# A 3x3 spatial convolution computed in pairs of rows: input-row sums on POOL, four products instead of six, combined on ACT and VectorE

## The chip, the core and the metric

The kernel runs on one core of a Trainium2 chip. A core has five engines with a queue of instructions each: PE (TensorE, matrix products), ACT (ScalarE), DVE (VectorE), POOL (GpSimd) and SP (SyncE, which here only issues DMA transfers). Each queue is worked off in order. PE reads SBUF and writes PSUM, a small memory of eight banks of 128 x 512 f32. The metric is the device time of one launch in microseconds (us).

## What is computed

Two layers work on x of shape (4, 128, 64, 64) in f32. Layer 0 is multi-head attention over the 4096 positions of each image, followed by a residual and a layer norm over channels. Layer 1 adds three branches of the result: a 3x3 convolution over 128 channels, a 1x1 product in the frequency domain, and a Mamba block (a selective scan over the positions).

```python
x = _L0_conv_ref(x, Wq, bq, Wk, bk, Wv, bv, Wo, bo, gamma, beta)   # 4 heads of 32, softmax over 4096 keys
spatial = jax.lax.conv_general_dilated(x, conv_spatial_w, (1, 1), ((1, 1), (1, 1)),
    dimension_numbers=('NCHW', 'OIHW', 'NCHW')) + conv_spatial_b[None, :, None, None]
ym = _mamba(u, in_proj_w, conv1d_w, conv1d_b, x_proj_w, dt_proj_w, dt_proj_b, A_log, D, out_proj_w)
...
return spatial + spectral + ym
```

The change concerns `spatial` alone.

## The kernel before

The work is cut into 32 chunks of 512 positions: a chunk is 8 rows of 64 of one image, held as 128 channels x 512. One Python loop writes the instructions of all engines in one order, in steps of a counter t. The attention takes 2048 steps: 64 halves (a half is a chunk of queries and a pair of heads) of 32 steps each, so that 64 steps belong to one chunk. In this document "step p" is the step with t mod 64 = p.

Each attention step issues to PE, in this order: six products into `s2` that end in the scores for the exponential (L496), four products into `s1` for the maxima of a later half (L455), then the products of other jobs, then two products of the exponentials of the step before with the values, `po` (L516). ACT takes the exponential of `s2` (L504, `e`), DVE reduces `s1` to maxima (L462, `part`). `s1` and `s2` have one buffer each of two banks, so that PE's next products into them wait for DVE and ACT. Every two steps there is also one state of the scan: ACT makes the decay `dA` (L829), POOL the input term `db` (L834), DVE scans (L846, `hs`), POOL multiplies by C and adds to an accumulator (L856, L875). On the last step of a half, `oz` (L526 on ACT, L527 on DVE) empties `po`. When the attention is over (`late`), the scan of the last chunks goes on alone, with `db` on DVE and the sum over states on PE (L882).

Everything else is a job: a generator that yields what it needs next, namely "P", "D" or "A" (a place on PE, DVE or ACT in this step), "B" (one of two PSUM banks), or "" (only the next step). `Plan.step` gives the places out by rank. An odd step has two places for each of PE, DVE and ACT, an even one has one place on ACT.

`convolve(c)` is such a job, of rank 3, queued at t0 + SLOT + 30. It takes one bank and issues nine products of 128 x 512, one per tap, with the padded input `xp` (10 rows of 66) read at an offset of dy rows and dx columns, one product per place "P". A tenth, `g_hil` with `hx`, adds a part of the spectral branch. Then ACT copies the bank to `ym` with the bias (L940). `scan_output` adds `ym` to the Mamba output about a chunk later (L997). `constants_of_the_rest` prepares the weights once: a part of the spectral 1x1 product is added to the middle tap.

The jobs of one chunk stand in the same steps from chunk to chunk. The products of `convolve` stand in steps 57, 59, 61, 63 and 1, two in each.

Of the kernel before, what the change touches and what calls it, by code (L numbers as in the profile page):

```python
# [9 lines left out]
F32 = mybir.dt.float32  # L10
F32R = mybir.dt.float32r
AF = mybir.ActivationFunctionType
ALU = mybir.AluOpType
# [4 lines left out]
P = 128  # L18
W = 64
# [5 lines left out]
RPC = L // W  # L25
# [136 lines left out]
def attention_then_conv_mamba(  # L162
# [17 lines left out]
    nc = tc.nc  # L180
# [8 lines left out]
    const = ctx.enter_context(tc.tile_pool(name="const", bufs=1))  # L189
    att = ctx.enter_context(tc.tile_pool(name="att", bufs=2))  # L190
    loc = ctx.enter_context(tc.tile_pool(name="loc", bufs=2))
# [9 lines left out]
    for h in range(HEADS):  # L201
        k, j = divmod(h, 2)
# [3 lines left out]
    for h in range(HEADS):  # L206
        k, j = divmod(h, 2)
        c = COL["bk"] + k
# [8 lines left out]
    for h in range(HEADS):  # L217
        k, j = divmod(h, 2)
        c = COL["bq"] + h
# [15 lines left out]
    nc.scalar.dma_start(vec, vecs)  # L235
    cw = const.tile([P, 9, P], F32, name="cw")
    nc.scalar.dma_start(cw, conv_w)
    inw = const.tile([P, 2 * DI], F32, name="inw")
    nc.scalar.dma_start(inw, in_w)

# [13 lines left out]
    def col(name, k=0):  # L254
        return vec[:, COL[name] + k : COL[name] + k + 1]
# [12 lines left out]
    g_flip, g_hil, g_fliphil = (g[:, k, :] for k in range(3))  # L268
# [8 lines left out]
    def constants_of_the_rest():  # L277


        yield ""  # L280
        half = loc.tile([P, 2, 2 * P], F32, tag="sg1", name="half", bufs=1)
        nc.vector.tensor_scalar(half, spw, 0.5, None, ALU.mult)
        rr, ir = half[:, 0, :P], half[:, 0, P:]
        ri, ii = half[:, 1, :P], half[:, 1, P:]
        yield ""
        g_id = loc.tile([P, P], F32, tag="ob", name="g_id", bufs=1)
        nc.gpsimd.tensor_tensor(g_id, rr, ii, ALU.add)
        nc.gpsimd.tensor_tensor(cw[:, 4, :], cw[:, 4, :], g_id, ALU.add)
        nc.gpsimd.tensor_tensor(g_flip, rr, ii, ALU.subtract)
        nc.gpsimd.tensor_tensor(g_hil, ri, ir, ALU.subtract)  # L290
        nc.gpsimd.tensor_tensor(g_fliphil, ri, ir, ALU.add)
        yield ""
        nc.vector.tensor_scalar(sbias, cst[:, K_G : K_G + W], col("spec_bi"), None, ALU.mult)
        nc.vector.tensor_tensor(sbias[:, 0:1], sbias[:, 0:1], col("spec_br"), ALU.add)
        high = loc.tile([4 * DTR, DI], F32R, tag="zg1", name="dtw_high", bufs=1)
        nc.vector.tensor_copy(high, dtw_f)
        nc.vector.scalar_tensor_tensor(dtw, high, less_w[: 4 * DTR], dtw_f, ALU.mult, ALU.add)

        nc.scalar.activation(negA, vec[:, COL["A_log"] : COL["A_log"] + NH * NS], AF.Exp)
        yield ""  # L300
        nc.vector.tensor_scalar(negA, negA, -1.0, None, ALU.mult)


        bank = yield "PB"
        pb = bank_tile(bank, [P, 1], "pb")
        nc.tensor.matmul(pb, Wo, bvc, start=True, stop=True)
        yield "D"
        plan.release(bank, 2)
        nc.vector.tensor_tensor(bo, pb, col("bo"), ALU.add)
# [18 lines left out]
    plan = Plan(2, {"x": 2, "f": 1})  # L328

    def bank_tile(bank, shape, name):  # L330
        return psum.tile(shape, F32, tag=f"m{bank}", name=name)
# [309 lines left out]
    xps, xss, dts, us, accs, gates, xds, bcds = ({} for _ in range(8))  # L641
# [245 lines left out]
    hxs, yms, edges, wd, ymd = {}, {}, set(), {}, {}  # L887
# [31 lines left out]
    def convolve(c):  # L919

        i = c % NCH
        while c not in edges or c not in hxs:
            yield ""
        bank = yield "PB"
        pf = bank_tile(bank, [P, RPC, W], f"pf_{c}")
        for k in range(9):
            if k:
                yield "P"
            dy, dx = divmod(k, 3)
            nc.tensor.matmul(  # L930
                pf, cw[:, k, :], xps[c][:, dy : dy + RPC, dx : dx + W], start=k == 0, stop=False
            )
        flat = pf.rearrange("p r w -> p (r w)")
        yield "P"
        nc.tensor.matmul(flat, g_hil, hxs.pop(c), start=False, stop=True)
        yield "A"
        plan.release(bank)
        ym = loc.tile([P, L], F32, tag="ym", name=f"ym_{c}", bufs=2)
        yms[c] = ym
        nc.scalar.activation(ym, flat, AF.Identity, bias=col("conv_b"))  # L940
        if i == 0:
            nc.gpsimd.tensor_tensor(ym[:, :W], ym[:, :W], sbias, ALU.add)

# [88 lines left out]
    for b in range(B):  # L1032
# [3 lines left out]
        for i in range(NCH):  # L1036
# [3 lines left out]
            plan.at(t0 + NT + 1 + i * TPC, 0, place_v(b, i))  # L1040
    plan.at(-20, 0, constants_of_attention())
    plan.at(-4, 2, constants_of_the_rest())
    for H in range(HALVES):
        if H % PAIRS == 0:
# [5 lines left out]
    for c in range(CHUNKS):  # L1050
        t0 = (c + 1) * SLOT
        plan.at(t0, 0, load_residual(c))
        plan.at(t0 + 16, 1, mamba_input(c))
        plan.at(t0 + SLOT + 30, 3, convolve(c))
        plan.at(c * SLOT + LAG + 6, 3, gate(c))
        plan.at((c + 1) * SLOT + LAG + (2 if c < CHUNKS - 3 else 6), 0, scan_output(c))
# [7 lines left out]
    while t < end or not plan.idle():  # L1064
# [10 lines left out]
        c, s = divmod(t - LAG, SLOT)  # L1075
# [110 lines left out]
```

## Time and profile before

| what | value |
|---|---|
| median of 3 runs | 6019.52 us (6018.47 to 6020.24) |
| the profiled execution | 6019.83 us, its span 6018.0 us, granted clock 0.987 |
| PE busy | 5827.6 us, 97% |
| DVE, ACT, POOL busy | 4292.9, 3550.9, 4481.7 us (71%, 59%, 74%) |
| first and last `e` (L504) | start at 132.3 us and 5796.7 us |
| one chunk (64 steps), middle of the span | 178.8 to 179.1 us |
| after the last `e` starts | 221.3 us, PE busy for 138.9 us of it, DVE 170.8 us, POOL 166.6 us |

Busy time of PE counts a product from its start to its modelled end; products overlap, so the pace is read from one start to the next. "PEld" is the load of weights, which overlaps PE. A line of the timeline gives start, duration, engine, source line, operation, tiles, shapes, the number of instructions merged into it and, in brackets, how long the engine had been idle and what ended that. An f32 product shows as two matrix instructions, each with its own load of weights.

### The profile page before, as it was taken

Reading aid. Unit: us, or ns where it says so; the run is one execution under the profiler, and the core shown is the slowest. Engines: PE = TensorE matmul, PEld = TensorE weight load, DVE = VectorE, ACT = ScalarE, POOL = GpSimd, SP = SyncE. Lnnn points to the kernel's source line nnn. Section 1 sums busy time; section 2 is a strip of 40 time slices with the busy share of each in tenths; the row PEclk is TensorE's granted clock in tenths of the full one; section 3 lists DMA queues with packets and bytes.
Section 4 is the critical chain, followed back from the end, with each engine's and each line's share of the span. In section 5 each row is a group of like instructions: output and inputs, shape, how many; then the busy total and the mean of one; then the engine's idle time right before and its main releaser. Section 6 shows DMA issues by size and latency. Waiting matters only on the chain. (4 is left out here: it accounts for less than half of the span.)

```text
span 6018.0 us, 83940 instructions
## 1 busy us (share of the span) xinstructions
PE 5827.6 (97%) x31126; PEld 2415.4 (40%) x31126; DVE 4292.9 (71%) x4505; ACT 3550.9 (59%) x4762; POOL 4481.7 (74%) x4523
## 2 busy tenths in 40 slices
PE   5999999999999999999999999999999999999976
PEld 2444444444444444444444444444444444444422
DVE  4557777777777777777777777777777777777657
ACT  1455666665666666666666666666566666666653
POOL 0006888778888777888787888877788887788887
PEclk7999999999999999999999999999999999999988
DMA  4012222323333222323433323322333222222233
GB/s 129 21 37 57 67 72 76 72 71 109 84 90 74 75 70 71 76 69 81 110 86 79 77 67 72 76 72 68 110 76 92 68 67 64 67 70 65 60 101 90
DMA packets 423320, 456.46 MB, mean 76 GB/s; under 512 B 203360, under 2 KB 204928, under 8 KB 422912
## 3 DMA queue, kind: packets, MB, share of 16 engines
q1 hardware_dynamic: 418256, 449.23, 29.4%
q8 instruction: 246, 4.03, 0.3%
q10 hardware_dynamic: 4656, 1.87, 0.1%
q14 instruction: 162, 1.33, 0.1%
HBM read 376.21 MB, written 66.32 MB: 74 GB/s over the span
## 5 line engine op out<-in xcount | busy, mean ns | idle before, releaser
L462 DVE TENSOR_REDUCE part<-s 128x2 f32<-128x1024 f32 x2048 | 2498.0, 1221 | 1460.7 <-PE s L455 1460.5
L504 ACT ACTIVATE e<-s 128x1024 f32<-128x1024 f32 x2048 | 2095.0, 1023 | 2176.7 <-PE s L496 2174.2
L516 PE MATMUL po<-e,V 128*33 128x512 f32 x8192 | 2181.9, 605 | 2.7 <-DVE oz L527 0.3
L496 PE MATMUL s<-Q,K 64*128 64x512 f32 x8192 | 1502.9, 444 | 8.8 <-ACT e L504 4.4
L455 PE MATMUL s<-K,Q 64*128 64x512 f32 x8192 | 1320.6, 400 | 47.8 <-DVE part L462 35.9
L856 POOL TENSOR_TENSOR hs<-hs,bc 128x512 f32<-128x512 f32 x948 | 1210.3, 1277 | 170.3 <-DVE hs L846 101.8
L496 PEld LDWEIGHTS s<-Q,K 64*128 64x128 f32 x8192 | 610.4, 185 | 1730.5 <-ACT e L504 1257.1
L834 POOL TENSOR_TENSOR db<-u,bc 128x512 f32<-128x512 f32 x948 | 1215.3, 1282 | 0.0
L875 POOL TENSOR_TENSOR acc<-acc,hs 128x512 f32<-128x512 f32 x894 | 1145.0, 1281 | 70.1
L846 DVE TENSOR_TENSOR_SCAN hs<-dA,state,db 128x512 f32<-128x512 f32 x826 | 1052.2, 1274 | 49.4 <-ACT dA L829 47.7
L455 PEld LDWEIGHTS s<-K,Q 64*128 64x128 f32 x8192 | 751.2, 186 | 313.3 <-DVE part L462 140.6
L496 PE MATMUL s<-MX,sel 64*128 64x512 f32 x4096 | 811.3, 392 | 0.0
L829 ACT ACTIVATE dA<-dt,negA 128x512 f32<-128x512 f32 x1024 | 703.0, 687 | 112.1 <-DVE V L846 69.5
L855 POOL COPY state<-hs 128x1 f32<-128x1 f32 x858 | 158.6, 185 | 769.3 <-DVE hs L846 769.1
L516 PEld LDWEIGHTS po<-e,V 128*33 128x33 f32 x8192 | 305.5, 109 | 906.9 <-issue 862.2
L496 PEld LDWEIGHTS s<-MX,sel 64*128 64x128 f32 x4096 | 386.3, 184 | 91.5 <-issue 0.3
L930 PE MATMUL pf<-xp,cw 128*128 128x512 f32 x576 | 288.8, 620 | 0.0
L560 POOL TENSOR_TENSOR op<-op,rz 128x512 f32<-128x512 f32 x32 | 41.7, 1303 | 184.0 <-DMA rz<-rd 184.0
L846 DVE TENSOR_TENSOR_SCAN hs<-dA,zero,db 128x512 f32<-128x512 f32 x128 | 163.0, 1274 | 0.3
L882 PE MATMUL acc<-V,cst 128*128 128x512 f32 x140 | 92.5, 761 | 64.2 <-POOL V L856 64.1
L930 PEld LDWEIGHTS pf<-xp,cw 128*128 128x128 f32 x576 | 97.0, 189 | 122.3 <-issue 120.9
L714 POOL TENSOR_TENSOR xs<-xs,sg_x 128x512 f32<-128x512 f32 x64 | 82.0, 1281 | 74.8 <-ACT sg_x L638 74.8
(143 smaller groups left out, 3392.8 us busy)
## 6 DMA issues: line engine op xcount, KB each, us to landing
bc<-bcd SPq DMA_DIRECT2D x487, 512.0 KB
Q<-qd SPq DMA_DIRECT2D x256, 128.0 KB
K<-kd SPq DMA_DIRECT2D x64, 256.0 KB
MX<-md SPq DMA_DIRECT2D x1024, 0.5 KB
K<-bcd SPq DMA_DIRECT2D x42, 256.0 KB
vd<-vst SPq DMA_DIRECT2D x32, 264.0 KB
V<-vd SPq DMA_DIRECT2D x32, 264.0 KB
xq<-in_x SPq DMA_DIRECT2D x32, 256.0 KB
```

What stands on the lines that cost most here:

```text
L455: nc.tensor.matmul(sc[:, j, :], QT[H][rows[j], n, t * P : (t + 1) * P], KK[k][m][rows[j], :], start=n == 0, stop=n == 1,)
L462: nc.vector.tensor_reduce(part[H][:, :, t, m], sc, AX.X, ALU.max)
L496: nc.tensor.matmul(s[:, j, :], sel[rows[j], :] if n == 2 else KK[k][i][rows[j], t * P : (t + 1) * P], mov[rows[j], :], start=n == 0, stop= ...
L504: nc.scalar.activation(e, s, AF.Exp)
L516: nc.tensor.matmul(po[H][used[j], :], VA[i][:, t, 2 * k + j, :], e[:, j, :], start=m == 0, stop=m == NT - 1,)
L829: nc.scalar.activation(dA[c, v], dts[c][hf], AF.Exp, scale=negA[:, k : k + 1])
L834: engine.tensor_tensor(db[c, v], us[c][hf], bcs[c, n][0], ALU.mult)
L846: nc.vector.tensor_tensor_scan(hs, dA.pop((c, v)), db.pop((c, v)), state[:, k : k + 1] if c % NCH else zero, ALU.mult, ALU.add,)
L855: nc.gpsimd.tensor_copy(state[:, k : k + 1], hs[:, L - 1 :])
L856: nc.gpsimd.tensor_tensor(hs, hs, bcs[c, n][1], ALU.mult)
L875: nc.gpsimd.tensor_tensor(accs[c, hf], accs[c, hf], hs, ALU.add)
L930: nc.tensor.matmul(pf, cw[:, k, :], xps[c][:, dy : dy + RPC, dx : dx + W], start=k == 0, stop=False)
```

## The change

The 3x3 convolution is rewritten so that each pair of output rows is made from four products of an input-row combination with a combination of the taps, instead of from six products of a row with a tap (three dx each). With input rows d0 to d3 of a pair and tap rows above, middle, below, the four are (d1 + d2) by (above + below + middle)/2, (d2 - d1) by (above + below - middle)/2, (d0 - d2) by above and (d1 - d3) by minus below. The even output row is the sum of the first three, the odd one is the first minus the second plus the fourth.

- Once, in `constants_of_the_rest`: one more step and six POOL instructions of 128 x 384 that make the combined taps in place and in `cw2`.
- Per chunk, on POOL: four additions or subtractions of 128 x 264 into a new tile `d` of one buffer, in two rounds of two (`outer` 0 and 1).
- On PE: twelve products of 128 x 256 instead of nine of 128 x 512, two per place "P", and the unchanged `g_hil` product, which now starts the second round. Each round takes a bank of its own after a wait of four steps.
- On ACT: one copy of 128 x 256 per chunk instead of one of 128 x 512.
- On DVE: four instructions of 128 x 256 per chunk, two after each round; the second pair adds the bias.

```diff
@@ -235,6 +235,7 @@
     nc.scalar.dma_start(vec, vecs)
     cw = const.tile([P, 9, P], F32, name="cw")
     nc.scalar.dma_start(cw, conv_w)
+    cw2 = const.tile([P, 3, P], F32, name="cw2")
     inw = const.tile([P, 2 * DI], F32, name="inw")
     nc.scalar.dma_start(inw, in_w)
 
@@ -289,6 +290,16 @@
         nc.gpsimd.tensor_tensor(g_flip, rr, ii, ALU.subtract)
         nc.gpsimd.tensor_tensor(g_hil, ri, ir, ALU.subtract)
         nc.gpsimd.tensor_tensor(g_fliphil, ri, ir, ALU.add)
+
+        yield ""
+        above, middle, below = (cw[:, 3 * k : 3 * k + 3, :] for k in range(3))
+        outer = loc.tile([P, 3, P], F32, tag="ym", name="outer", bufs=2)
+        nc.gpsimd.tensor_tensor(outer, above, below, ALU.add)
+        nc.gpsimd.tensor_tensor(cw2, outer, middle, ALU.subtract)
+        nc.gpsimd.tensor_tensor(middle, outer, middle, ALU.add)
+        nc.gpsimd.tensor_scalar(cw2, cw2, 0.5, None, ALU.mult)
+        nc.gpsimd.tensor_scalar(middle, middle, 0.5, None, ALU.mult)
+        nc.gpsimd.tensor_scalar(below, below, -1.0, None, ALU.mult)
         yield ""
         nc.vector.tensor_scalar(sbias, cst[:, K_G : K_G + W], col("spec_bi"), None, ALU.mult)
         nc.vector.tensor_tensor(sbias[:, 0:1], sbias[:, 0:1], col("spec_br"), ALU.add)
@@ -921,23 +932,55 @@
         i = c % NCH
         while c not in edges or c not in hxs:
             yield ""
-        bank = yield "PB"
-        pf = bank_tile(bank, [P, RPC, W], f"pf_{c}")
-        for k in range(9):
-            if k:
-                yield "P"
-            dy, dx = divmod(k, 3)
-            nc.tensor.matmul(
-                pf, cw[:, k, :], xps[c][:, dy : dy + RPC, dx : dx + W], start=k == 0, stop=False
-            )
-        flat = pf.rearrange("p r w -> p (r w)")
-        yield "P"
-        nc.tensor.matmul(flat, g_hil, hxs.pop(c), start=False, stop=True)
-        yield "A"
-        plan.release(bank)
+
+
+
+        d0, d1, d2, d3 = (xps[c][:, r : r + RPC - 1 : 2, :] for r in range(4))
         ym = loc.tile([P, L], F32, tag="ym", name=f"ym_{c}", bufs=2)
+        by_row = ym.rearrange("p (a b w) -> p b a w", b=2, w=W)
+        for outer in range(2):
+            d = loc.tile([P, 2, RPC // 2, W + 2], F32, tag="d", name=f"d_{c}_{outer}", bufs=1)
+            if outer:
+                nc.gpsimd.tensor_tensor(d[:, 0], d0, d2, ALU.subtract)
+                nc.gpsimd.tensor_tensor(d[:, 1], d1, d3, ALU.subtract)
+                taps = cw[:, 0:3, :], cw[:, 6:9, :]
+            else:
+                nc.gpsimd.tensor_tensor(d[:, 0], d1, d2, ALU.add)
+                nc.gpsimd.tensor_tensor(d[:, 1], d2, d1, ALU.subtract)
+                taps = cw[:, 3:6, :], cw2
+            for _ in range(4):
+                yield ""
+            bank = yield "PB"
+            pf = bank_tile(bank, [P, 2, RPC // 2, W], f"pf_{c}_{outer}")
+            if outer:
+                hx = hxs.pop(c).rearrange("p (a b w) -> p b a w", b=2, w=W)
+                nc.tensor.matmul(pf, g_hil, hx, start=True, stop=False)
+            for q in range(6):
+                k, dx = divmod(q, 3)
+                if outer and q == 0 or q and q % 2 == 0:
+                    yield "P"
+                nc.tensor.matmul(
+                    pf[:, k],
+                    taps[k][:, dx, :],
+                    d[:, k, :, dx : dx + W],
+                    start=dx == 0 and not outer,
+                    stop=q == 5 or dx == 2 and not outer,
+                )
+            if not outer:
+                yield "A"
+                nc.scalar.activation(by_row[:, 1], pf[:, 1], AF.Copy)
+            yield "D"
+            plan.release(bank, 2)
+            if outer:
+                for k in range(2):
+                    y = by_row[:, k]
+                    nc.vector.scalar_tensor_tensor(
+                        y, pf[:, k], col("conv_b"), y, ALU.add, ALU.add
+                    )
+            else:
+                nc.vector.tensor_tensor(by_row[:, 0], pf[:, 0], by_row[:, 1], ALU.add)
+                nc.vector.tensor_tensor(by_row[:, 1], pf[:, 0], by_row[:, 1], ALU.subtract)
         yms[c] = ym
-        nc.scalar.activation(ym, flat, AF.Identity, bias=col("conv_b"))
         if i == 0:
             nc.gpsimd.tensor_tensor(ym[:, :W], ym[:, :W], sbias, ALU.add)
 
```

## The prediction

> **What bounds the kernel now.** I read the page first: the engines' busy shares and the group of the products that the change replaces.
>
> ```profile
> PE 5827.6 (97%) x31126; PEld 2415.4 (40%) x31126; DVE 4292.9 (71%) x4505; ACT 3550.9 (59%) x4762; POOL 4481.7 (74%) x4523
> L930 PE MATMUL pf<-xp,cw 128*128 128x512 f32 x576 | 288.8, 620 | 0.0
> ```
>
> PE is busy nearly all the time, and before the products of the convolution it never waits. But busy PE is a modelled figure, so I went to PE's timeline next, in the middle of a chunk.
>
> ```profile
> 3115.94 1.05 PE L516 MATMUL po<-e,V 128*33 128x512 f32 x4
> ...
> 3118.29 1.05 PE L516 MATMUL po<-e,V 128*33 128x512 f32 x4
> ...
> 3120.64 1.99 PE L930 MATMUL pf<-xp,cw 128*128 128x512 f32 x4
> 3122.55 1.05 PE L516 MATMUL po<-e,V 128*33 128x512 f32 x4
> ...
> 3241.77 1.16 PE L895 MATMUL p<-cst,xh 128*128 128x128 f32 x8
> 3242.86 1.05 PE L516 MATMUL po<-e,V 128*33 128x512 f32 x4
> ```
>
> From `po` to `po` a step without jobs takes 2.35 us. With a group of two f32 products (four instructions) it takes 4.26. So a group of the convolution costs 3122.55 - 3120.64 = 1.91 us of the span, in full: in this stage PE sets the pace. The last two lines show a group of eight narrow instructions of 128 columns, which costs 1.09.
>
> Third, I looked for what happens in steps where PE has no job to do but the other engines do. The boundary between the two halves of a chunk (steps 32 to 35) is such a place. First ACT's timeline, then DVE's and PE's:
>
> ```profile
> 3223.79 1.02 ACT L504 ACTIVATE e<-s 128x1024 f32<-128x1024 f32 x1 [1.25 <-PE s L496]
> ...
> 3234.24 1.02 ACT L504 ACTIVATE e<-s 128x1024 f32<-128x1024 f32 x1 [0.85 <-PE s L496]
> ```
>
> ```profile
> 3225.85 0.69 DVE L527 COPY oz<-po 33x512 f32<-33x512 f32 x1 [0.39 <-ACT oz L526]
> ...
> 3229.03 0.73 PE L455 MATMUL s<-K,Q 64*128 64x512 f32 x4 [0.47 <-DVE part L462]
> ```
>
> Four steps last 10.45 us here and not 4 x 2.35 = 9.40: 1.05 us is lost, because DVE must take `oz` and job work between two maxima, and PE then waits for DVE before it can refill `s1`. The other boundary of a chunk (steps 0 to 3) has the same `oz`, but there products of the convolution stand before and behind it, and nothing is lost.
>
> **The change on PE.** Between starts an instruction of 512 columns takes 0.429 us (L930) and one of 128 columns 0.112 (L895). A group's cost is that times its number plus 0.195 (1.91 - 4 x 0.429, and 1.09 - 8 x 0.112 gives the same). For 256 columns the line through both gives 0.218. In the built order all other PE jobs keep their steps. The convolution has four groups now: eight half-wide instructions in step 57 (1.94 us), four in 59 (1.07), `g_hil` and four in step 7 (1.93), eight in 9 (1.94); together 6.88 against 5 x 1.91 = 9.55. That is 2.67 us per chunk. The convolutions of chunks 0 to 28 lie wholly inside the attention, so 29 x 2.67 = 77 us if nothing else becomes late. Of chunk 29 only the first eight products lie inside: 4 x 1.91 - 1.94 - 1.07 = 4.6 us.
>
> A rule speaks against this. In the Trainium skill, "TensorE: Matmul & The Clock Gate", section "Back-to-back issue gap", the sustained pace of load-and-multiply pairs is about 81 ns at 128 columns and 131 at 512: narrow products gain little, since the weight load sets a floor. By it a half-wide instruction would cost about 0.75 of a full one (0.32 us) and the sum would be 6040 us. The rows here, 0.112 at 128 columns against 0.429, disagree with it.
>
> **The change on the other engines, per chunk.** POOL: four `d` operations of 264 columns. A POOL TENSOR_TENSOR of 128 columns takes 0.456 us (L289), one of 512 takes 1.28 (L768); by the line 0.75, from start to start 0.70: 2.8 us. The first pair is issued at step 53 and the steps 57 to 61 leave POOL idle for 2.7 us each, so it costs nothing. The second pair comes behind `u` of step 1, in POOL's fullest stretch. From 3306.28 to 3337.24 (steps 61 to 7) POOL is idle only twice:
>
> ```profile
> 3320.70 1.28 POOL L856 TENSOR_TENSOR hs<-hs,bc 128x512 f32<-128x512 f32 x1 [2.77 <-DVE hs L846]
> ...
> 3337.24 1.28 POOL L856 TENSOR_TENSOR hs<-hs,bc 128x512 f32<-128x512 f32 x1 [1.02 <-DVE hs L846]
> ```
>
> In those steps three groups disappear (5.7 us) and 1.4 us of work is added. POOL, which multiplies `hs` 2.5 us after the scan at step 2 (3328.49 against 3326.0), will be about 2.5 + 1.4 + 5.7 - 0.9 - 2.77 = 6 us late. The scan that waits is the one of step 6, whose `db` stands behind that; between the two lie about 10.5 us, and POOL needs 6 and then 1.35 + 1.24 + 1.24 for product, sum and `db`. It just fits. What is a little late then is hidden by the new group of step 7, 1.93 us, and by step 9 POOL is level. If that cover were gone, the excess would be paid in full. Queued behind POOL are also the `bc` loads on SP, which wait for the same products (2832.7 us in all in SP's waits) and have their rows loaded three states ahead, over 11 us of POOL's work.
>
> ACT: 681 ns per chunk (L940) give way to a copy of half the width, between 257 ns (64 columns, L674) and 592 (512 columns, L913); I take 0.4. It stands between `oz` of step 0 and the exponential of step 1.
>
> DVE: four operations of 256 columns. From start to start L612 takes 0.32 (128 columns) and L997 0.595 (512 columns with a PSUM input); by the line 0.41, 1.65 per chunk. The last two stand in step 11, where DVE idles 1.12 us before the next maxima: no cost. The first two stand behind the maxima and `dt` of step 1, and there is the one cost that I charge. From the maxima of step 0 (3317.00) DVE has 5.3 us of work until it has finished `dt` (3322.3), where two steps without their cover offer 4.70. With 0.82 more the maxima of step 2 start 1.4 us late. The slack of `s1` is 0.46 (maxima at 3224.23 end at 3225.46, PE's next turn comes 2.35 us after 3223.57), so PE loses 0.94. The boundary at step 32, which has no cover today, loses 1.05. I take 0.95. ACT's queue in steps 61 to 2 is 12.2 us for 14.1, dense only within odd steps, and I charge it nothing beyond this.
>
> So a chunk gains 2.67 - 0.95 = 1.72 us, 29 chunks 49.9.
>
> The preparation adds six POOL instructions of 128 x 384, 0.456 to 1.28 us each, 3 to 8 us in all, at about 127 us, where POOL has nothing for hundreds of us (21.7 us busy from 150 to 500). If that cover were gone it would be 8 us. Its extra step moves `bo` by one step, needed far later. Both: 0.
>
> **The end.** Behind the attention DVE sets the pace, with 1.92 us per state. The convolution stops it today:
>
> ```profile
> 5966.83 0.69 ACT L940 ACTIVATE ym<-pf,vec 128x512 f32<-128x512 f32 x1 [7.69 <-PE pf L935]
> ...
> 5968.13 1.28 DVE L846 TENSOR_TENSOR_SCAN V<-dA,state,db 128x512 f32<-128x512 f32 x1 [5.14 <-ACT dA L829]
> ```
>
> ACT waits for ten products, and the next `dA` stands behind it. After the change DVE itself waits, twice per chunk: for six half-wide products and a copy (2.6 + 0.5 us) and for `g_hil` and six (3.5 us), each less the 1.92 us of a state that runs beside it and plus what PE still has queued, 1.5 to 3 and 1.5 to 2.5. Add 1.65 of DVE work: 4.7 to 7.2 against about 5. For chunks 29 to 31 that is -2 to +8 us; I take +3.
>
> **The sum.** 6019.8 (the profiled execution, 0.3 above the median of the runs) - 49.9 - 4.6 + 3 = 5968 us.
>
> **The rivals.**
> 1. The cover isn't missed: ACT and DVE catch up within the pairs of steps, and the whole 2.67 comes through. For it: over each pair of steps DVE and ACT have less work than time. Against it: the 1.05 us at step 32. 6019.8 - 77 - 4.6 = 5938.
> 2. All uncovered pairs of steps lose as much as the worst pair does today (steps 32 and 33 take 5.25 instead of 4.70: 0.55). Five such pairs, 59 to 4, take 2.75 us and the gain of 2.67 is gone, with POOL's lateness as the likeliest cause. 6019.8 + 2 - 4.6 + 3 = 6020. Against it: pairs with two or three ACT jobs, such as 5 and 6, lose 0.16.
> 3. Slower: the weight loads come out. Each f32 instruction has its own load, 189 ns (PEld L930), hidden under 429 ns of the one before. Half-wide ones offer 214. If half of each load is not covered, an instruction costs 0.218 + 0.095 = 0.313, the groups sum to 9.2 us, 0.4 is gained where 0.95 is lost, and the time is 6019.8 + 16 - 3.5 + 3 = 6035. It decides from 0.29 us per instruction on. (The page named above states a floor of this kind.) Against it: at 128 columns the same loads of 192 ns follow each other every 112 ns.
>
> **Chances.** The forecast's case 0.60 (5950 to 5992, with 0.6 to 1.2 lost per chunk and the end's bounds), the first rival 0.18, the second 0.12, the third 0.06, and 0.04 for a mishap that I don't see. A measurement of this kernel can tell about 0.2%, 12 us, from no change. The second rival is spread around no change (0.07 the same, 0.02 faster, 0.03 slower). Faster by over 0.2%: 0.60 + 0.18 + 0.02 = 0.80; the same 0.08; slower 0.12. The range, 5933 to 6002, holds the forecast's case, nearly all of the first rival and a part of the second.
>
> **What would show it.** PE instructions of the convolution 0.21 to 0.23 us apart; groups of 1.9, 1.1, 1.9 and 1.9 us in steps 57, 59, 7 and 9; a chunk of 177.3 us where it was 179.0; PE's wait for the maxima in steps 1 and 2 near 1 us; no scan waiting for POOL's `db` by more than 1 us; `d` operations of 0.75 us. The forecast is wrong if the instructions are 0.29 us apart or more, if chunks still take 178.5 us or more, or if the part behind the last exponential grows by over 10 us.

## The result and the profile after

| what | before | after |
|---|---|---|
| median of the timed runs | 6019.88 us (4 runs) | 5973.11 us (4 runs, 5970.53 to 5976.93) |
| ratio | 1 | 0.9921, 95% interval 0.9904 to 0.9939 |
| the profiled execution | 6019.83 us | 5976.93 us (the longest of its four), span 5975.1 us, granted clock 0.985 |
| first `e` to last `e` | 5664.3 us | 5612.0 us |
| behind the last `e` | 221.4 us | 230.3 us |
| a chunk in the middle of the span | 179.0 us | 177.6 us |
| a chunk of the last image | 177.3 us | 174.7 us |

The forecast was 5968 us, the median is 5973.11: the change gains 46.8 us in the medians. Between the two profiled executions it gains 42.9, because the one after is 3.8 us above its median. Of these, the attention gets 52.4 us shorter, the part behind the last `e` 8.9 us longer, and the first `e` starts 0.6 us later. The page after, with the lines that answer to those shown of before (busy time and share of each engine; then the group of the products):

```profile
PE 5766.0 (96%) x31318; PEld 2461.1 (41%) x31318; DVE 4343.8 (73%) x4633; ACT 3535.4 (59%) x4762; POOL 4575.5 (77%) x4657
...
L962 PE MATMUL pf<-d,cw 128*128 128x256 f32 x768 | 199.1, 396 | 7.3 <-POOL d L944 7.3
```

The products went from 576 instructions and 288.8 us of modelled busy time to 768 and 199.1. What they cost of the span is read from starts, in PE's timeline at steps 57 and 59 of one chunk and at step 9 of the next:

```profile
3272.48 1.99 PE L962 MATMUL pf<-d,cw 128*128 128x256 f32 x8
3274.40 1.05 PE L527 MATMUL po<-e,V 128*33 128x512 f32 x4
...
3279.09 1.13 PE L962 MATMUL pf<-d,cw 128*128 128x256 f32 x4
3280.16 1.05 PE L527 MATMUL po<-e,V 128*33 128x512 f32 x4
...
3317.67 2.00 PE L962 MATMUL pf<-d,cw 128*128 128x256 f32 x8
3319.60 1.05 PE L527 MATMUL po<-e,V 128*33 128x512 f32 x4
```

The groups cost 1.92, 1.07 and 1.93 us where 1.94, 1.07 and 1.94 were forecast. DVE's and PE's timelines between these, in steps 0 to 2, show where a part of it is lost again:

```profile
3292.18 1.23 DVE L473 TENSOR_REDUCE part<-s 128x2 f32<-128x1024 f32 x1 [1.26 <-PE s L466]
3293.80 0.69 DVE L538 COPY oz<-po 33x512 f32<-33x512 f32 x1 [0.39 <-ACT oz L537]
3294.52 1.28 DVE L857 TENSOR_TENSOR_SCAN hs<-dA,state,db 128x512 f32<-128x512 f32 x1
3295.72 1.20 DVE L473 TENSOR_REDUCE part<-s 128x2 f32<-128x1024 f32 x1
3296.84 0.68 DVE L777 SCALAR_TENSOR_TENSOR dt<-dt,lnw 128x512 f32<-128x512 f32 x1
3297.43 0.42 DVE L981 TENSOR_TENSOR ym<-pf,ym 128x256 f32<-128x256 f32 x1
3297.89 0.42 DVE L982 TENSOR_TENSOR ym<-pf,ym 128x256 f32<-128x256 f32 x1
3298.23 1.22 DVE L473 TENSOR_REDUCE part<-s 128x2 f32<-128x1024 f32 x1
```

```profile
3293.62 0.40 PE L507 MATMUL s<-MX,sel 64*128 64x512 f32 x2
3293.86 0.62 PE L466 MATMUL s<-K,Q 64*128 64x512 f32 x4
...
3296.10 0.40 PE L507 MATMUL s<-MX,sel 64*128 64x512 f32 x2
3296.98 0.74 PE L466 MATMUL s<-K,Q 64*128 64x512 f32 x4 [0.48 <-DVE part L473]
```

PE waits (3296.98) for the maxima of step 1 (3295.72), not for those of step 2. From the start of the last products into `s2` (L507) to the first into `s1` (L466) it takes 0.24 us in step 0 and 0.88 in step 1, so PE is 0.64 us late there. From the maxima of step 0 to those of step 1 DVE needs 3.54 us, where a step lasts 2.35: it waits 0.39 us for ACT's half of `oz`, copies its own half, and scans. `dt` and the new pair come only behind that. The starts of `e`, median over the middle chunks, give the price: steps 1 and 2 take 5.76 us, and two steps without a job take 4.70. In the kernel before they took 6.68 with a group of 1.91 in step 1, so 4.77. The kernel before has the same 3.54 us between these maxima (3317.00 and 3320.54), but there the group of 1.91 us keeps PE busy over it.

The end, in DVE's timeline, for the last chunk:

```profile
5922.76 0.42 DVE L981 TENSOR_TENSOR ym<-pf,ym 128x256 f32<-128x256 f32 x1 [2.94 <-ACT ym L971]
...
5936.37 0.88 DVE L977 SCALAR_TENSOR_TENSOR ym<-pf,vec,ym 128x256 f32<-128x256 f32 x2 [3.13 <-PE pf L962]
```

DVE stands still twice for one convolution, as forecast. For chunk 30 the two waits are 4.08 and 6.76 us.

### The profile page after: what moved, and what is told of

Read it like the earlier page. It is cut to its first block, busy times and chain, and to the rows that moved or that the text cites. A ratio compares the mean times of both kernels' runs of the same rounds, so it can differ in the third digit from the quotient of the medians.

```text
span 5975.1 us, 84571 instructions
## 1 busy us (share of the span) xinstructions
PE 5766.0 (96%) x31318; PEld 2461.1 (41%) x31318; DVE 4343.8 (73%) x4633; ACT 3535.4 (59%) x4762; POOL 4575.5 (77%) x4657
## 5 line engine op out<-in xcount | busy, mean ns | idle before, releaser
L507 PE MATMUL s<-Q,K 64*128 64x512 f32 x8192 | 1502.4, 444 | 12.7 <-ACT e L515 5.7
L466 PE MATMUL s<-K,Q 64*128 64x512 f32 x8192 | 1327.9, 401 | 57.8 <-DVE part L473 46.0
L507 PEld LDWEIGHTS s<-Q,K 64*128 64x128 f32 x8192 | 610.4, 185 | 1737.9 <-ACT e L515 1290.3
L466 PEld LDWEIGHTS s<-K,Q 64*128 64x128 f32 x8192 | 751.8, 186 | 330.4 <-DVE part L473 165.4
L507 PE MATMUL s<-MX,sel 64*128 64x512 f32 x4096 | 815.4, 393 | 0.0
L507 PEld LDWEIGHTS s<-MX,sel 64*128 64x128 f32 x4096 | 391.2, 184 | 93.9
L962 PE MATMUL pf<-d,cw 128*128 128x256 f32 x768 | 199.1, 396 | 7.3 <-POOL d L944 7.3
L962 PEld LDWEIGHTS pf<-d,cw 128*128 128x128 f32 x768 | 141.1, 193 | 73.0 <-issue 47.4
```

The lines of the kernel that those rows point to most:

```text
L466: nc.tensor.matmul(sc[:, j, :], QT[H][rows[j], n, t * P : (t + 1) * P], KK[k][m][rows[j], :], start=n == 0, stop=n == 1,)
L507: nc.tensor.matmul(s[:, j, :], sel[rows[j], :] if n == 2 else KK[k][i][rows[j], t * P : (t + 1) * P], mov[rows[j], :], start=n == 0, stop= ...
L962: nc.tensor.matmul(pf[:, k], taps[k][:, dx, :], d[:, k, :, dx : dx + W], start=dx == 0 and not outer, stop=q == 5 or dx == 2 and not outer,)
```

## The experiments

All ratios are to the kernel before, timed beside each version (medians of 6019.2 to 6022.8 us). "Steps 1, 2" is the time of these two steps together, less the products of the convolution in step 1 where there are any (1.91 or 1.07 us).

| version | median, us | ratio, 95% interval | chunk | steps 1, 2 | steps 32 to 35 |
|---|---|---|---|---|---|
| before | 6019.88 | 1 | 179.02 | 4.77 | 10.45 |
| after | 5973.11 | 0.9921 (0.9904 to 0.9939) | 177.56 | 5.76 | 10.46 |
| before_gap | 6034.14 | 1.0020 (1.0011 to 1.0029) | 179.80 | 5.76 | 10.46 |
| after_61 | 5973.03 | 0.9919 (0.9905 to 0.9933) | 177.41 | 5.76 | 10.46 |
| after_63 | 5947.42 | 0.9877 (0.9863 to 0.9890) | 176.11 | 4.74 | 10.45 |
| after_tail | 5964.15 | 0.9903 (0.9888 to 0.9918) | 177.55 | 5.76 | 10.46 |
| after_oz | 5948.98 | 0.9879 (0.9865 to 0.9892) | 176.49 | 4.89 | 9.63 |
| before_oz | 6010.56 | 0.9980 (0.9971 to 0.9989) | 178.86 | 4.78 | 9.63 |
| after_nopair | 5972.44 | 0.9918 (0.9903 to 0.9931) | 177.51 | 5.76 | 10.46 |
| after_nosum | 5973.87 | 0.9918 (0.9904 to 0.9932) | 177.57 | 5.76 | 10.46 |
| after_oz_narrow | 5919.01 | 0.9834 (0.9821 to 0.9848) | 175.65 | 4.89 | 9.57 |
| before_oz_narrow | 5982.96 | 0.9941 (0.9928 to 0.9953) | 178.02 | 4.78 | 9.57 |
| oz_tail | 5910.41 | 0.9819 (0.9806 to 0.9832) | 175.65 | 4.89 | 9.57 |
| oz_tail_63 | 5902.27 | 0.9806 (0.9792 to 0.9819) | 175.13 | 4.76 | 9.57 |

### Moving the products

before_gap:

```diff
         for k in range(9):
+            if k == 4:
+                for _ in range(9):
+                    yield ""
             if k:
                 yield "P"
```

> The kernel before, with a pause of nine steps between the fourth and the fifth product of the convolution: the groups stand in steps 57, 59, 5, 7 and 9 and no longer in 61, 63 and 1. No engine gets any work that it did not have. Theory (the loss in steps 61 to 2 comes from the missing cover alone): what the changed kernel loses there, 1.24 us per chunk, is lost here too, 0.9 to 1.3 per chunk, 27 to 39 us in all: 6047 to 6059 us. Rival (the loss comes from the sums on POOL and the new instructions on DVE): there are none here, so 6020 us within 5.

It took 12.4 us more than the kernel before beside it, less than half of what the theory said. Its steps show why: in steps 1 and 2 the loss is there at its full size, 0.99 us, with no new work on any engine. The timelines of DVE and PE there:

```profile
3151.17 0.69 DVE L527 COPY oz<-po 33x512 f32<-33x512 f32 x1 [0.39 <-ACT oz L526]
3151.90 1.28 DVE L846 TENSOR_TENSOR_SCAN hs<-dA,state,db 128x512 f32<-128x512 f32 x1
3153.10 1.20 DVE L462 TENSOR_REDUCE part<-s 128x2 f32<-128x1024 f32 x1
```

```profile
3154.36 0.73 PE L455 MATMUL s<-K,Q 64*128 64x512 f32 x4 [0.48 <-DVE part L462]
```

The groups that moved to steps 5, 7 and 9 found holes of their own: steps 7 and 8, which lost 0.28 us before (4.98 for 4.70), take 6.60 with a group of 1.91, so 4.69; steps 5 and 6 took 4.86 and now take 4.71 without their group. I had not counted that. A chunk ends up 0.78 us longer and the attention 18.3 us, while the part behind the last `e` is 4.0 us shorter in the profiled executions (217.4 for 221.4), which I have not explained. The rival, no loss without new work, is out.

after_61 and after_63 (the number is 56 in the first and 58 in the second):

```diff
         while c not in edges or c not in hxs:
             yield ""
+        while not plan.late and 30 <= plan.t % SLOT < 56:
+            yield ""
```

> The kernel after, with the first round of products in steps 61 and 63 in place of 57 and 59; the second round stays in 7 and 9, and POOL, ACT and DVE have the same work. Theory: the groups stand again where oz and dt make DVE late; of the 1.24 us that a chunk loses in steps 61 to 2 at least 0.6 and at most all come back, so a chunk takes 176.3 to 177.0 us where it takes 177.6, and the time is 5937 to 5956 us. Rival: POOL's sums stand where they stood, so nothing changes: 5973 us within 5.

> The kernel after, with the first round of products in steps 63 and 1 and the second in 9 and 11; the copy on ACT and the first pair on DVE move to about step 3, the second POOL pair behind them. Theory: the larger group now stands right before oz and the smaller one right behind; step 61 loses its cover (0.3 us at most) and the first DVE pair leaves step 1. A chunk takes 176.2 to 176.9 us, the time is 5934 to 5954 us, at or a little below that of the version with 61 and 63. Rival: 5973 us within 5.

after_61 changed the time by nothing that can be told apart (a chunk is 0.15 us shorter), and so my theory in its first form fell: groups in front of `oz` cover nothing of the loss behind it. The time is the one that the rival named, and whether POOL's sums are the reason is left to after_nosum below. Steps 57 to 60, which lost their groups, take 9.44 us for 9.40, steps 61 to 0, which got them, take 12.37 with 2.99 of products, so 9.38 for 9.57, and step 1 keeps its whole loss. after_63 came out as expected, but for a narrower reason. Its group of four instructions stands in step 1 itself. PE's timeline there:

```profile
3099.73 1.13 PE L964 MATMUL pf<-d,cw 128*128 128x256 f32 x4
3100.79 1.05 PE L527 MATMUL po<-e,V 128*33 128x512 f32 x4
...
3102.58 0.63 PE L466 MATMUL s<-K,Q 64*128 64x512 f32 x4
```

Step 1 takes 3.63 us with that group and 3.64 without. The 1.07 us of products are free: they fill the time in which PE would wait for the maxima, and 3102.58 has no wait. Steps 7 and 8, where no products stand any more, lose nothing either (4.69 us). 1.07 + 0.28 and 0.1 in small changes elsewhere are the 1.45 us that a chunk gained. This edit moves ACT's copy, the pair on DVE and the second round too; but before_gap, which has neither copy nor pair, lost the same 0.99 us.

That gave theory 2: the loss is one event, the maxima of step 1 behind `oz` and a scan. Step 33 has the same event: in the kernel before DVE takes the maxima of step 32 at 3224.23, then `oz` and a scan, then those of step 33 at 3227.77, again 3.54 us. The time from L507 to L466, median over the middle chunks, marks both places: it is 0.23 us in a plain step, 0.88 in step 1 of the kernel after, 0.87 in step 1 of before_gap and 0.86 in step 33 of both; in step 1 of the kernel before and of after_63 it is 0.23.

### What stands ahead of the maxima

after_oz, and the same edit on the kernel before:

```diff
-                po[H][used[j], :],
-                VA[i][:, t, 2 * k + j, :],
+                po[H][used[j], :] if j else po[H][:HS, :],
+                VA[i][:, t, 2 * k + j, :]
+                if j
+                else VA[i][:, t, 2 * k : 2 * k + 2, :].rearrange("p h d -> p (h d)")[:, :HS],
...
-            nc.scalar.activation(oz[H][used[0], :], p[used[0], :], AF.Identity)
-            nc.vector.tensor_copy(oz[H][used[1], :], p[used[1], :])
+            nc.scalar.activation(oz[H][: HS + HD + 1, :], p[: HS + HD + 1, :], AF.Identity)
```

> The kernel after, without DVE's part of oz: one ACT instruction of 97 rows empties po in place of one of 33 rows on ACT and one of 33 on DVE; so that these rows are all written, the products of the first head of a pair write 64 rows instead of 33. Theory 2 (formed on the runs with moved groups: PE waits in step 1 for the maxima of step 1, which come late because oz and a scan stand ahead of them on DVE; the same happens at step 32): both losses go, 1.06 us at step 1 and 1.1 at steps 32 to 35. Over 32 chunks 55 to 67 us: 5906 to 5918 us. Rival A (the prediction's own step: dt and the new DVE pair delay the maxima of step 2): step 32 gains its 1.1, step 1 keeps a third to a half of its loss: 5925 to 5940. Rival B (POOL): step 1 keeps its loss, 5935 to 5940.

> The kernel before with the same edit of oz. Theory 2: in step 1 a group of the convolution covers oz already, so that only the loss at steps 32 to 35 goes, 1.05 to 1.15 us in each of 32 chunks, and in the last image's six chunks a further 0.8 at step 1: 5978 to 5988 us. The change is then worth its whole time on PE, 65 to 75 us between the two kernels with this edit, where it is 47 without. Rivals A and B: the same here, but the two kernels stay 47 to 60 us apart.

after_nopair:

```diff
+        if not plan.late:
+            nc.gpsimd.memset(by_row[:, 0], 0.0)
         for outer in range(2):
...
-            else:
+            elif plan.late:
                 nc.vector.tensor_tensor(by_row[:, 0], pf[:, 0], by_row[:, 1], ALU.add)
                 nc.vector.tensor_tensor(by_row[:, 1], pf[:, 0], by_row[:, 1], ALU.subtract)
```

> The kernel after without the two DVE instructions behind the first round while the attention runs (the first three terms of the output rows are then missing); in their place POOL clears the even rows in step 30. Theory 2: these two stand behind the maxima of step 1 and delay only those of step 2, which have room: step 1 stays at 3.6 us, the time is 5968 to 5974 us. Rival A (the prediction's own step): DVE is 0.8 us less late, step 1 or 2 gets 0.6 to 0.9 us shorter in each of 24 chunks: 5951 to 5959 us.

after_nosum:

```diff
-                nc.gpsimd.tensor_tensor(d[:, 0], d0, d2, ALU.subtract)
-                nc.gpsimd.tensor_tensor(d[:, 1], d1, d3, ALU.subtract)
+                d = d0, d3
...
-                nc.gpsimd.tensor_tensor(d[:, 0], d1, d2, ALU.add)
-                nc.gpsimd.tensor_tensor(d[:, 1], d2, d1, ALU.subtract)
+                d = d1, d2
...
-                    d[:, k, :, dx : dx + W],
+                    d[k][:, :, dx : dx + W],
```

> The kernel after without the sums on POOL: the products read single rows of the padded input where they read d (each sum of two rows is replaced by its first row or so). Theory 2: step 1 stays at 3.6 us; what POOL's lateness costs is at most the 0.27 us of step 7 and some of the part behind the attention: 5960 to 5973 us. Rival B (POOL's sums are the cause of the loss in steps 61 to 2): a chunk takes 176.5 us where it takes 177.56, and the time is 5935 to 5945 us.

The last two settle the rivals. after_nopair leaves the pair out, after_nosum the four sums. Neither moves a chunk by more than 0.05 us, and steps 1 and 2 keep their 5.76 us (after_nosum is 0.9 us above what I expected). The pair on DVE and the sums on POOL cost the attention nothing.

The oz edit took the loss away at both places, as theory 2 says: 0.87 us at steps 1 and 2 and 0.83 at steps 32 to 35 in the kernel after, only the second in the kernel before. But both times came out too long, by 31 us and 23 us against the edges of what I expected, and their distance, 61.6 us, lies between the 65 to 75 of theory 2 and the 47 to 60 of the rivals. Every plain step had become longer, 2.365 us for 2.345. The groups of `po` in the trace of after_oz (busy time, mean ns of one) show the wider form:

```profile
L527 PE MATMUL po<-e,V 128*64 128x512 f32 x4096 | 2194.2, 617 | 0.1
L527 PE MATMUL po<-e,V 128*33 128x512 f32 x4096 | 2143.5, 605 | 0.0
```

So I kept 64 rows for the first product of each half alone:

```diff
+            wide = m == 0 and j == 0
...
+                po[H][:HS, :] if wide else po[H][used[j], :],
+                VA[i][:, t, 2 * k : 2 * k + 2, :].rearrange("p h d -> p (h d)")[:, :HS]
+                if wide
+                else VA[i][:, t, 2 * k + j, :],
```

> As the version of the kernel after with oz on ACT alone, but only the first product of a half writes 64 rows (which is enough for all rows to be written once); the others write 33 again. In that version a plain step takes 2.37 us where it took 2.34 to 2.35, and the first product into po 0.643 us where it took 0.618. Theory 2 with that as a cost of the edit itself (0.66 us per chunk, 21 us): 5928 us, 5922 to 5934, a plain step back at 2.34 to 2.35, step 1 at 2.8, steps 32 to 35 at 9.5 to 9.6 together. If the cost has another source (97 rows on ACT): 5949 us within 5.

> The kernel before with the same edit. Theory 2: 5990 us, 5984 to 5996. Between this one and the same edit on the kernel after there should then be the change's whole PE time less the small losses of steps 7 and 61 to 0 and the longer end: 58 to 70 us where the two kernels of the change differ by 47. If they differ by 47 or less, the boundary at step 1 was not where the expected gain went.

The plain step is back at 2.345 us, and the kernel after comes to 5919.01 us, 30 us less than with the wide products (3 us beyond the lower edge of what I expected; before_oz_narrow is 1 us beyond). DVE's timeline in steps 0 to 2 of after_oz_narrow:

```profile
3085.49 1.23 DVE L473 TENSOR_REDUCE part<-s 128x2 f32<-128x1024 f32 x1 [1.28 <-PE s L466]
3086.63 1.27 DVE L859 TENSOR_TENSOR_SCAN hs<-dA,state,db 128x512 f32<-128x512 f32 x1
3087.83 1.23 DVE L473 TENSOR_REDUCE part<-s 128x2 f32<-128x1024 f32 x1
3088.97 0.68 DVE L779 SCALAR_TENSOR_TENSOR dt<-dt,lnw 128x512 f32<-128x512 f32 x1
```

From maxima to maxima it is 2.34 us now, with the scan between them and `dt` behind them as ever. PE's waits for maxima over the whole span, of the kernel after first and of after_oz_narrow second (total, times, longest):

```profile
PE s L466 <- DVE part L473: 46.0, 88, 1.3
```

```profile
PE s L466 <- DVE part L473: 21.2, 33, 1.3
```

Of the 88 waits 30 fall in step 1 (14.3 us) and 28 in step 33 (13.0 us); of the 33 one falls in step 1 (0.4 us) and none in step 33, and from L507 to L466 it is 0.23 us at both places. Of what is left 18.0 us fall in step 63, in both kernels alike. These records do not hold the whole of the 53.5 us that the attention got shorter: where PE is 0.64 us late, 0.48 shows as a wait. No run moves the scan; with `oz` out of the way and the scan still there, 0.19 us is lost in steps 1 and 2 (4.89 for 4.70).

With that wait away the change is worth 5982.96 - 5919.01 = 64 us, where it was worth 46.8. A chunk differs by 2.37 us (178.02 - 175.65), most of what the products save.

### The end

```diff
             if not outer:
+                for _ in range(3 if plan.late else 0):
+                    yield ""
                 yield "A"
                 nc.scalar.activation(by_row[:, 1], pf[:, 1], AF.Copy)
+            for _ in range((3 if outer else 2) if plan.late else 0):
+                yield ""
             yield "D"
```

> The kernel after, changed behind the attention alone: three more job steps between the first round's products and ACT's copy, two between the copy and DVE's pair, three between the second round's products and DVE's second pair, so that PE has finished when they come up in their queues. Theory (DVE waits in order for PE and ACT, 2.94 and 3.13 us in the last chunk and so for the others): the attention stays at 5612 us, the part behind the last exponential shrinks from 230 to 219 to 225 us, and the time is 5962 to 5968 us. Rival (it is the work that DVE got, three chunks of 1.7 us, and the POOL sums before it): 5973 us within 3.

It took 9.0 us less than the kernel after; the attention is the same (5612.9 us) and the part behind the last `e` fell from 230.3 to 219.9. (The granted clock there differs too, 0.78 and 0.81, so I go by the medians, whose runs don't overlap.) The same instructions of the last chunk in DVE's timeline of after_tail:

```profile
5921.80 0.42 DVE L985 TENSOR_TENSOR ym<-pf,ym 128x256 f32<-128x256 f32 x1
...
5939.67 0.87 DVE L981 SCALAR_TENSOR_TENSOR ym<-pf,vec,ym 128x256 f32<-128x256 f32 x2
```

Neither waits now, and DVE does the same work behind the last `e` (175.6 us busy, 174.5 in the kernel after). The end was longer because of the order, not because of the work.

### Together

> The kernel after with both oz edits (ACT alone, 64 rows in the first product only) and the later places of ACT's copy and DVE's instructions behind the attention. The two gains lie in different parts of the span and should add: 5928 less 9, 5912 to 5926 us.

> As the one before, and the products' first round in steps 63 and 1, the second in 9 and 11. Theory 2: with oz gone there is little left in step 1 for a group to fill, so that of the 1.45 us per chunk that these places gained without the oz edit only the 0.27 of step 7 and what is still lost in step 1 (0.4) come: 0.3 to 0.7 us in 24 chunks, 7 to 17 us: 5902 to 5912 us. Rival (the places gain by themselves, whatever oz does): the whole 26 us, 5893.

oz_tail is 2 us below what was expected: the end again gives 8.6 us. oz_tail_63 is as expected, at the lower edge: the places in steps 63 and 1 give 8.1 us where they gave 25.7 without the oz edit. What they gained was mostly the wait that oz made. oz_tail_63 is the best version, 5902.27 us: 1.94% under the kernel before (interval 1.81 to 2.08%) and 71 us under the kernel after.

## Why the prediction was right, and where it was not

**Products on PE: right.** Instructions of 256 columns follow each other every 216 ns (median; 218 was forecast), the groups (medians 1.92, 1.06, 1.92, 1.92) sum to 6.83 us for 6.88, and the gain of 2.67 us per chunk was 2.72. The third rival would have needed 0.29 us and more. By the figures of the Trainium skill, "TensorE: Matmul & The Clock Gate", section "Back-to-back issue gap", an instruction would cost about 0.32 us, which is an estimate. The trace does not agree with these figures for these products.

**The loss by the missing cover: the size nearly right, the step and the cause wrong.** I charged 0.95 us per chunk because `dt` and the new DVE pair would make the maxima of step 2 late by 1.4 us. The loss in steps 1 and 2 is 0.99 (5.76 - 4.77), 1.26 with what is lost next to them (2.72 less the 1.46 that a chunk gained), but it falls on the maxima of step 1, made late by `oz` and the scan. after_nopair shows that the pair has no part in it. The row that I set beside it, the 1.05 us at step 32, is the same event, which is why the number came out near: that was luck. The timeline that I read it from also shows the maxima of step 1 (3320.54) 3.54 us behind those of step 0, and I passed over them. PE's wait, for which I named about 1 us as a sign, is recorded as 0.48, in step 1. I also took all products from step 61 on as cover; after_61 and after_63 show that only the ones in step 1 cover this loss; those in steps 61 and 63 cover 0.19 us next to it (9.57 less 9.38).

**So the sum over chunks came out near because two errors offset each other.** In the first three images a chunk gains 1.46 us where I had 1.72. In the last image it gains 2.57, since there the products stood in steps 55 to 63 before, and step 1 had no cover to lose: it took 2.85 us before and 2.94 after, with no products in either. I had taken all 29 chunks as alike. 52.4 us in all against 54.5.

**POOL: right in what matters.** The trace shows POOL late by the forecast amount, `hs` of step 2 at 3305.98, 5.4 us behind the end of its scan at 3300.63 (6 were forecast):

```profile
3304.55 0.77 POOL L944 TENSOR_TENSOR d<-xp 128x264 f32<-128x264 f32 x1
3305.26 0.77 POOL L945 TENSOR_TENSOR d<-xp 128x264 f32<-128x264 f32 x1
3305.98 1.29 POOL L867 TENSOR_TENSOR hs<-hs,bc 128x512 f32<-128x512 f32 x1
```

But "no scan waiting for `db` by more than 1 us" missed. DVE's waits have this line (total, times, longest):

```profile
DVE hs L857 <- POOL db L845: 24.6, 27, 2.6
```

It costs the attention nothing that the runs could show: without the sums (after_nosum) this line falls to 2.2 us in 3 times, and a chunk is as long. What the sums cost behind the last `e` stays open: that part takes 223.0 us in the profiled execution of after_nosum, 230.3 in the kernel after, but the medians are level (5973.87 and 5973.11). The 0.27 us that steps 7 and 8 lose is in the kernel before too (0.28), so the new group there did not hide it either, as I had said it would. And the first pair of sums runs in step 32, not in 53: the job starts in step 30 and then waits for a bank until 57. POOL had room in both places.

**The end: the term that was mis-sized.** +3 us was taken from bounds of -2 to +8; it is +8.9 in the profiled executions. The mechanism, DVE waiting twice per convolution, is right. The sum of its terms is not: 2.6 + 0.5 and 3.5, each less 1.92, with 1.5 to 3 and 1.5 to 2.5 of queued work and 1.65 on DVE, give 7.4 to 9.9 us per convolution and not 4.7 to 7.2. Against the 5 us of before that is +7 to +15 for three. The terms themselves mostly hold. They make the two waits 2.7 to 4.2 and 3.1 to 4.1 us; the last chunk shows 2.94 and 3.13, chunk 30 shows 4.08 and 6.76, and chunk 29 next to nothing (0.32). About 3 us of the 6.76 go with the clock of that execution: from 5841 to 5847 us the granted clock is 0.50, and the twelve products of that round (5843.48) take 4.82 us, where those of the last chunk (5933.58) take 2.75. In after_61 the same wait is 3.79, at a granted clock of 1.00. after_tail gives what the two waits cost in the medians: 9.0 us.

**Preparation: 0 forecast,** the first `e` starts 0.6 us later.

The first rival (nothing lost, 5938; its sum leaves out the 3 us of the end that the others have) was wrong for this kernel, but is nearly what the change is worth once oz is out of the way. The second (the whole gain lost again) is out by the 1.46 us that a chunk gained, and POOL as its cause by after_nosum.

## What to carry to other kernels

Products taken off a busy PE bring their time only where no other wait stands under them: go through the steps that lose work one by one, and ask in each which instruction PE would wait for next and what stands ahead of that in its queue. A hole of the same kind elsewhere in the trace gives the price, but not the place; a run that moves the work by a few steps gives the place. If the wait is found, taking it away (here one copy off DVE) helps at every place where it stands, here two in a chunk and 54 us, and covering it only at one, here 26 us; and instructions that read fresh products on an engine that sets the pace should stand a few steps behind them.

## What the hardware showed that was not expected

The second pair of sums on POOL takes longer than the first for the same size: the first, L948 and L949, takes 643 and 650 ns, the second, L944 and L945, 758 and 757 (medians). It is not the step: in after_61 and after_63 the first pair runs in steps 58 and 60 (medians of 643 to 655 ns) and the second in steps 3 to 10 (749 to 759), and behind the attention, where other work stands around both, the first takes 642 to 653 and the second 747 to 756 in the kernel after, but for one instruction of each above 1 us. Nor addition against subtraction: the first pair is one of each. What goes with it is the distance of the two inputs, one row of 66 against two. No run isolates it.

Writing 64 rows instead of 33 in half of the products of `po` makes the first of them 0.643 us instead of 0.617 and a plain step 0.02 us longer. Taking it back out of all but the first products of a half brought 30 us of the 54 that separate after_oz_narrow from the kernel after.

Behind the last `e`, where PE is busy 144.8 of 230.3 us, the granted clock falls to 0.50 for stretches (0.78 in the mean). In one of them f32 instructions of 256 columns follow each other every 0.43 us, twice the 0.216 of the attention. In after_61 the same products fall outside of such a stretch.
